# Attention with a residual: the place of the token loads in the transfer queue, and two exponentials ahead of a copy in one cycle

## The chip, the cores and the metric

The kernel runs on one core of a Trainium2 chip. The core's engines run side by side, each through its own list of instructions in order, and wait for each other through semaphores: TensorE (PE, matmuls; its weight loads are listed apart as PEld), VectorE (DVE), ScalarE (ACT), GpSimd (POOL) and SyncE (SP), which here only issues transfers (DMAs). The metric is the device time of one execution in microseconds (us). "Before" is the kernel without the change.

## What is computed

64 sequences of 128 tokens with 512 channels go through one attention block with 16 query heads and one shared key/value head of 64 channels, plus a null key and value, an additive bias per head, a causal mask and a padding mask. All is float32. Cut to what matters:

```python
xn = layernorm(x, g_in)
q = (xn @ Wq).reshape(b, n, H, DH).transpose(0, 2, 1, 3) * scale
kv = xn @ Wkv
k, v = (kv[..., :DH], kv[..., DH:])
k = concat([nk, k], axis=1); v = concat([nv, v], axis=1)
sim = einsum('bhid,bjd->bhij', q, k) + bias
sim = where(causal_mask, neg, sim); sim = where(mask_p, sim, neg)
attn = softmax(sim, axis=-1)
out = einsum('bhij,bjd->bhid', attn, v)
out = out.transpose(0, 2, 1, 3).reshape(b, n, INNER) @ Wo
return x + layernorm(out, g_out)
```

## The kernel before

The sequences are worked on in pairs. A hand-written prologue handles the first ones; then `cycle(c)` runs for c = 1 to 29, and a hand-written ending follows. In cycle c three things are interleaved: the softmax of the pair 2c and 2c + 1 (`scores_max`, `exps`, `rinv`, `scale`, `blocks_T`), the output product of the pair before (`values_out`, `out_sum`, `out_one`), and the layer norm and residual of the pair before that (`pair_...`, `store`). Query products (`q_one`, and from cycle 2 on `leaf`) and the key/value product (`key_values`) of later sequences fill TensorE. A cycle ends with `region(c)`: the scores of the next pair (line 651), `values` of the present pair (line 770), then the additions of scores and bias on VectorE. The matmuls of queries and outputs are lines 597, 553 and 860, those of keys and values line 358.

The order of every engine is the order in which the calls are written; nothing is rescheduled. `nc.tensor.addr_align` places TensorE's code at a set offset in each cycle.

The input tokens of a group of four sequences go through these steps. Their layer norm is applied on ScalarE (`norm_apply`), VectorE transposes them in blocks of 32 (`tokens_T`, into `xb`), and at the end of each even cycle up to 26 `tokens_out` stores `xb` to a buffer in main memory (`xd`, 1 MB, line 340) and `tokens_in` loads it back in another layout as `xT` (four loads of 256 KB, line 348). `xT` is read first by `key_values` in the odd cycle after it (line 358, `pkv`), later by the query products. Two buffers take turns for `xT`.

Also in the even cycles, `values_send` has VectorE transpose the values of a group (`vt`, line 384) and stores them to main memory (`vd`, two stores of 64 KB, line 387), and `keys_send` copies the keys to the upper half of the partitions (`kT`, 128 KB, line 393). `values_fetch` loads the values as `vr` (line 399) in the odd cycle that follows. `load_res` loads the tokens of one sequence for the residual (`res`, 256 KB, line 138) and `load_mask` a padding mask (line 145).

All of these transfers are issued by SyncE, in the order in which they are written, and an issue that must wait holds back those behind it. The program gives its transfers eight completion counters in turn (`DMAHW0` to `DMAHW7` in the order of instructions); an issue also waits until the transfer that had its counter last has landed.

In cycle 1 alone (c below `LEAF`, which is 2) the query products take another way: `q_one(c, 6, 0)` adds a product to a bank of PSUM (tag `a`) and `keep` copies it out on ScalarE (`ku`, line 608); `q_one(c, 7, 0)` then adds another to the same bank, and `q_one(c, 4, 0)` another, copied by line 614. `exps` (line 701) runs one exponential per head row of `S`, on ScalarE, each with a sum that is read out by an accumulator instruction.

Of the kernel before, what the change touches and what calls it, by code (L numbers as in the profile page):

```python
# [17 lines left out]
def kernel(  # L18
# [67 lines left out]
    GB = 4  # L86
# [257 lines left out]
    def tokens_in(g):  # L344
        xT[g] = gp.tile([P, GB, KC, N], FP, tag="xT", name=f"xT_{g}")
        xd = xds.pop(g).rearrange("(i p) j e -> j p i e", p=Q)
        for j in range(NQ):
            nc.sync.dma_start(
                out=xT[g][j * Q : (j + 1) * Q].rearrange("p i c n -> p i (c n)"),
                in_=xd[j],  # L350
            )
# [39 lines left out]
    def keys_send(g):  # L391

        nc.sync.dma_start(out=kT[g][DH:], in_=kT[g][:DH])
# [22 lines left out]
    def q_tile(g, fp):  # L416

        for h in range(2):
            slot = 2 * fp + h if g % 2 == 0 else fp + 2 * h
            qT[g, fp, h] = gp.tile(  # L420
                [P, FH, GH, NQ, 2, Q], FP, tag=f"q{slot}", name=f"qT_{g}_{fp}_{h}", bufs=1
            )

    def q_part(g, c, h):

        f = c % NF
        return qT[g, f // FH, h][:, f % FH, :, :, c // NF, :]
# [66 lines left out]
    LEAF = 2  # L494
# [4 lines left out]
    def by_block(tag):  # L499
        return prod[tag].rearrange("p (t i q) -> p t i q", t=2, i=NQ)  # L500

    def first_into(g, c, h):
        nc.scalar.copy(q_part(g, c, h), by_block("a"))  # L503
# [77 lines left out]
    def product(g, f, k, pool, tag, start=True):  # L581

        if start:
            prod[tag] = pool.tile([P, HT], FP, tag=tag, name=f"p{tag}_{g}_{f}_{k}")
        lo, hi = xT[g][:, 0 : GB // 2], xT[g][:, GB // 2 :]
        t1, t2, t3, t4 = (xS.get((g, i)) for i in range(1, 5))
        w, t = {
            1: (a11, lo[:, :, lo_k]),
            2: (a12, lo[:, :, hi_k]),
            3: (s4, hi[:, :, hi_k]),  # L590
            4: (a22, t4),
            5: (s1, t1),
            6: (s2, t2),
            7: (s3, t3),
        }[k]
        for kc in range(HK):
            nc.tensor.matmul(  # L597
                prod[tag],
                w[:, kc, f * P : (f + 1) * P],
                t[:, :, kc, :],  # L600
                start=(start and kc == 0),
                stop=(kc == HK - 1),
                skip_group_check=not start,
            )

    def keep(tag, name):
        kept[name] = bp.tile([P, HT], FP, tag=f"k{name}", name=f"k{name}", bufs=1)
        nc.scalar.copy(kept[name], prod[tag])

    def q_out(g, c, toks, tag, name=None):  # L610
        o = q_part(g, c, toks.start // HT)
        p = prod[tag].rearrange("p (t i q) -> p t i q", t=2, i=NQ)
        if name is None:
            nc.scalar.copy(o, p)
        else:
            k = kept.pop(name).rearrange("p (t i q) -> p t i q", t=2, i=NQ)
            nc.vector.tensor_tensor(o, p, k, ALU.add)
# [43 lines left out]
    def scores_upper(b, pool, tags):  # L661
        if len(tags) == 1:
            ps = pool.tile([P, 2, NF, N], FP, tag=tags, name=f"ps_{b}_1")
            heads(b, 1, [ps[:, r] for r in range(2)])
            pss[b, 1] = [(slice(0, R8), ps)]
        else:
            ps = [pool.tile([P, NF, N], FP, tag=t, name=f"ps_{b}_1{r}") for r, t in enumerate(tags)]
            heads(b, 1, ps)
            pss[b, 1] = [(slice(r * NF, (r + 1) * NF), ps[r]) for r in range(2)]

    def scores_lower(bs):
        low = [
            ps_q.tile([P, 2, NF, NL], FP, tag="ac"[r], name=f"ps_{bs[0]}_0{r}")
            for r in range(2)
        ]
        for k, b in enumerate(bs):
            heads(b, 0, [low[r][:, k] for r in range(2)])
            pss[b, 0] = [(slice(r * NF, (r + 1) * NF), low[r][:, k]) for r in range(2)]
# [3 lines left out]
    def scores_add(b, hf):  # L682
        for ks, ps in pss.pop((b, hf)):
            sv = S[b][:, ks, KEYS[hf]]
            if ks.stop - ks.start == R8:
                sv = sv.rearrange("p (r f) j -> p r f j", r=2)
            nc.vector.tensor_tensor(sv, ps, sv, ALU.add)  # L687

    def scores_max(b, hf):
        if hf == 0:  # L690
            nmax[b] = small.tile([P, 2, R8], FP, tag="nmax", name=f"nmax_{b}")
        nc.vector.tensor_reduce(  # L692
            nmax[b][:, hf], S[b][:, :, WITH_NULL[hf]], AX.X, ALU.max, negate=True
        )

    def exps(b, hf, lo=0, hi=R8):
        if hf == 0 and lo == 0:
            rsum[b] = small.tile([P, 2, R8], FP, tag="rsum", name=f"rsum_{b}")
        for k in range(lo, hi):
            row = S[b][:, k, WITH_NULL[hf]]  # L700
            nc.scalar.activation(  # L701
                row,
                row,
                AF.Exp,
                bias=nmax[b][:, hf, k : k + 1],
                accum_out=rsum[b][:, hf, k : k + 1],
            )
# [46 lines left out]
    def values(bs):  # L754
        banks = value_banks(bs[0])
        for k, b in enumerate(bs):
            values_one(b, k, banks)
# [222 lines left out]
    def q_one(c, k, h):  # L980
        i = 2 * c + 4 + h
        g, f = divmod(i, GB)
        if g >= NG:
            return
        if k == 1 and f % FH == 0:
            q_tile(g, f // FH)
        if k == 1:
            product(g, f, 1, ps_q, "a")
            if c >= LEAF:
                first_into(g, f, 0)  # L990
            else:
                keep("a", "p1")
        elif k == 2:
            product(g, f, 2, ps_w, "w")
            q_out(g, f, lo_t, "w", "p1")
        elif k == 5:
            product(g, f, 5, ps_q, "c")
        elif k == 6:
            product(g, f, 6, ps_q, "a", start=False)
            if c >= LEAF:  # L1000
                first_into(g, f, 1)
            else:
                keep("a", "u2")
        elif k == 7:
            product(g, f, 7, ps_q, "a", start=False)
            if c >= LEAF:
                first_into(g, HC + f, 0)
            else:
                keep("a", "u3")
                q_out(g, HC + f, hi_t, "c", "u3")  # L1010
        elif k == 8:
            nc.vector.tensor_tensor(
                q_part(g, HC + f, 1), by_block("c"), q_part(g, HC + f, 0), ALU.add
            )
            o = q_part(g, f, 1)
            nc.vector.tensor_tensor(o, by_block("c"), o, ALU.add)
        elif k == 3:
            product(g, f, 3, ps_q, "c", start=False)
            q_out(g, f, hi_t, "c", "u2")
        else:  # L1020
            product(g, f, 4, ps_q, "a", start=False)
            q_out(g, HC + f, lo_t, "a")
# [34 lines left out]
    def region(c):  # L1057
        b0, b1, n0, n1 = (2 * c + i for i in range(4))
        if n0 < B:
            scores_upper(n0, ps_s, "s")  # L1060
            scores_lower((n0, n1))
            scores_upper(n1, ps_w, "ww")
        if 0 <= b0 < B:
            values((b0, b1))
        if n0 < B:
            scores_add(n0, 1)
            scores_add(n0, 0)
            if c < 0:
                scores_max(n0, 0)
                scores_max(n0, 1)  # L1070
            scores_add(n1, 0)
            scores_add(n1, 1)
# [5 lines left out]
    def cycle(c):  # L1078
        b0, b1, n0, n1 = (2 * c + i for i in range(4))
        p, r, m = b0 - 2, b0 - 4, b0 + 10  # L1080
        soft, nxt = b0 < B, n0 < B
        pair, fin, toks = 0 <= p < B, 0 <= r < B, m < B
        first, more = c % 2 == 0, 2 * c + 4 < B
# [46 lines left out]
            q_one(c, 2, 0)  # L1130
        if c >= LEAF:
            leaf(c, 2, 0)
        q_one(c, 6, 0)
        if soft:
            exps(b0, 0)
        out_one(p, 1)
        if c % 2 and n0 < B:
            mask_neg(n0 // GB)
# [139 lines left out]
            tokens_out(m // GB)  # L1278
        if c >= LEAF:
            leaf(c, 3, 3)  # L1280
        if first and toks:
            tokens_in(m // GB)
        if pair:
            load_res(p)
        if first and send < NG:
            values_send(send)
            keys_send(send)
        region(c)


# [166 lines left out]
    for c in range(1, B // 2 - 2):  # L1457
        cycle(c)
# [186 lines left out]
```

## Time and profile before

| what | value |
|---|---|
| three runs | 1028.63, 1030.47, 1030.57 us (median 1030.47) |
| the profiled execution | 1028.7 us |
| its span, first to last instruction | 1026.9 us |
| mean granted TensorE clock | 0.998 |
| instructions | 31794 |
| ScalarE and GpSimd busy | 643.4 us (63%) and 790.5 us (77%) |
| VectorE busy | 854.6 us (83%) |
| transfers | 100.91 MB, mean 98 GB/s |

The profile is one execution, written by the hardware profiler. A row of a timeline or a group has the start in us from the span's start, the duration, the engine, the line of the kernel, the operation, the tile that is written and those that are read, and in brackets the time that the engine was idle before it and what ended that. "SPq" is SyncE's issue of a transfer: its duration is that of the issue, not of the transfer. A row of a stretch has the stretch, its length, then busy time and count of PE, PEld, DVE, ACT and POOL, the granted clock, the share of the transfer engines and GB/s. Queue q8 and q14 carry the engines' own instructions, q1 SyncE's transfers; a row of a queue has its packets, MB and the share of 16 transfer engines' time in the window asked for.

### The profile page before, as it was taken

How to read it: one execution, taken by the hardware profiler on the slowest of the kernel's cores; microseconds unless marked ns; L12 is line 12 of the kernel's file. 1: busy time of each engine (PE TensorE's matmuls, PEld its weight loads, DVE VectorE, ACT ScalarE, POOL GpSimd, SP SyncE). 2: the span in 40 equal slices, each digit the busy share in tenths (PEclk: the TensorE clock that was granted, in tenths of full speed). 3: DMA queues.
4: the chain of work that ended last, by engine and by line, in shares of the span. 5: the costliest groups of instructions: out<-in, count | busy, mean ns of one | idle time of the engine just before them, and what ended most of it. 6: DMA issues, size and time to landing. Idle time of an engine off the chain costs nothing. (4 is left out here: it accounts for less than half of the span.)

```text
span 1026.9 us, 31794 instructions
## 1 busy us (share of the span) xinstructions
PE 1011.5 (98%) x12104; PEld 898.8 (88%) x12104; DVE 854.6 (83%) x2000; ACT 643.4 (63%) x2742; POOL 790.5 (77%) x710
## 2 busy tenths in 40 slices
PE   8999999999999999999999999999999999999997
PEld 7888888888888899888889888898888898888876
DVE  6776888988888898888888889888888988778798
ACT  2655776555775556765557765557765567755591
POOL 3798959688695877968689596886968789596874
PEclk9999999999999999999999999999999999999999
DMA  6551251624314252241523505244151521402203
GB/s 212 164 128 52 95 126 40 160 64 134 106 39 142 64 154 87 80 121 43 168 74 99 132 32 158 64 125 115 44 153 48 157 85 72 109 26 68 84 2 103
DMA packets 70264, 100.91 MB, mean 98 GB/s; under 512 B 27744, under 2 KB 31328, under 8 KB 68320
## 3 DMA queue, kind: packets, MB, share of 16 engines
q1 hardware_dynamic: 69008, 97.83, 33.0%
q8 instruction: 96, 1.57, 0.7%
q10 hardware_dynamic: 1104, 1.05, 0.3%
q14 instruction: 56, 0.46, 0.2%
HBM read 63.19 MB, written 33.55 MB: 94 GB/s over the span
## 5 line engine op out<-in xcount | busy, mean ns | idle before, releaser
L701 ACT ACTIVATE s<-s,nmax 128x65 f32<-128x65 f32 (+1 forms) x1024 | 379.2, 409 | 3.5 <-DVE nmax L692 3.5
L701 ACT ACTIVATION_READ_ACCUMULATOR s<-s,nmax 128x1 f32 x1024 | 238.1, 233 | 0.0
L722 POOL TENSOR_TENSOR s<-s,rinv 128x1024 f32<-128x1024 f32 (+1 forms) x128 | 189.8, 1484 | 45.7 <-DVE rinv L718 45.7
L635 POOL TENSOR_TENSOR s<-biasp,mneg 128x1552 f32<-128x1552 f32 x64 | 205.1, 3224 | 2.6 <-DMA x<-in_x_dram 2.0
L810 ACT ACTIVATE oT<-poX,nv 128x256 f32<-128x256 f32 x58 | 27.6, 475 | 224.5 <-PE poX L770 117.5
L687 DVE TENSOR_TENSOR s<-ps,s 128x256 f32<-128x256 f32 (+2 forms) x224 | 120.0, 605 | 15.7 <-PE ps L651 15.2
L556 DVE TENSOR_TENSOR qT<-pl,qT 128x128 f32<-128x128 f32 (+1 forms) x420 | 122.5, 323 | 2.7 <-PE pl L553 2.3
L860 PE MATMUL pyX<-wo,oT 128*128 128x256 f32 x512 | 121.4, 380 | 0.0
L692 DVE TENSOR_REDUCE nmax<-s 128x8 f32<-128x520 f32 (+1 forms) x128 | 116.5, 949 | 0.1
L860 PE MATMUL pyX<-wT,oT 128*128 128x256 f32 x488 | 115.6, 380 | 0.7 <-POOL oT L843 0.7
L737 DVE STREAM_TRANSPOSE sb<-s 128x1536 f32<-128x1536 f32 x64 | 113.2, 1768 | 0.6 <-POOL s L722 0.6
L860 PEld LDWEIGHTS pyX<-wo,oT 128*128 128x128 f32 x512 | 96.9, 190 | 14.3 <-issue 0.9
L917 POOL TENSOR_TENSOR rstdo<-rstdo,nhalf 128x1 f32<-128x1 f32 x64 | 35.1, 550 | 86.5 <-DVE rstdo L913 86.5
L860 PEld LDWEIGHTS pyX<-wT,oT 128*128 128x128 f32 x488 | 88.3, 190 | 10.9 <-POOL oT L843 1.1
L651 PE MATMUL ps<-kT,qT 64*64 64x128 f32 (+1 forms) x4096 | 93.6, 245 | 0.7 <-issue 0.7
L651 PEld LDWEIGHTS ps<-kT,qT 64*64 64x64 f32 x4096 | 85.5, 134 | 5.7 <-issue 2.4
L770 PE MATMUL pos<-sb,vr 32*64 32x128 f32 (+1 forms) x1792 | 84.6, 322 | 2.1 <-issue 1.7
L843 POOL TENSOR_TENSOR yS<-oT 128x512 f32<-128x512 f32 x32 | 41.2, 1288 | 50.6 <-ACT oT L810 47.0
L770 PE MATMUL poY<-sb,vr 32*64 32x128 f32 x720 | 77.4, 349 | 0.0
L770 PE MATMUL poX<-sb,vr 32*64 32x128 f32 x960 | 75.6, 301 | 0.0
L718 DVE RECIPROCAL rinv<-rsum 128x8 f32<-128x8 f32 x128 | 23.8, 187 | 54.3 <-ACT s L701 54.2
L503 ACT COPY qT<-pa 128x256 f32<-128x256 f32 x168 | 67.9, 404 | 1.1 <-PE pa L597 1.1
(150 smaller groups left out, 2561.3 us busy)
## 6 DMA issues: line engine op xcount, KB each, us to landing
res<-in_x_dram SPq DMA_DIRECT2D x64, 256.0 KB, 3.0
out_dram<-y SPq DMA_DIRECT2D x58, 256.0 KB, 2.1
x<-in_x_dram SPq DMA_DIRECT2D x224, 64.0 KB, 2.0
xd<-xb SPq DMA_DIRECT2D x14, 1024.0 KB, 4.5
xT<-xd SPq DMA_DIRECT2D x56, 256.0 KB, 5.5
vr<-vd SPq DMA_DIRECT2D x64, 128.0 KB, 3.2
x<-in_x_dram SPq DMA_DIRECT2D x8, 256.0 KB, 4.8
vd<-vt SPq DMA_DIRECT2D x32, 64.0 KB, 5.9
```

Source lines behind the costliest of these rows:

```text
L503: nc.scalar.copy(q_part(g, c, h), by_block("a"))
L556: nc.vector.tensor_tensor(o, p, o, ALU.add)
L635: nc.gpsimd.tensor_tensor(S[b], biasp, mneg[:, t].unsqueeze(1).broadcast_to([P, R8, ROW]), ALU.add,)
L651: nc.tensor.matmul(to[r][i * DH : (i + 1) * DH, f, :], qT[g, f // FH, t // GH][rows, f % FH, t % GH, NQ - 1 - i if hf else i], kT[g][rows, ...
L687: nc.vector.tensor_tensor(sv, ps, sv, ALU.add)
L692: nc.vector.tensor_reduce(nmax[b][:, hf], S[b][:, :, WITH_NULL[hf]], AX.X, ALU.max, negate=True)
L701: nc.scalar.activation(row, row, AF.Exp, bias=nmax[b][:, hf, k : k + 1], accum_out=rsum[b][:, hf, k : k + 1],)
L722: nc.gpsimd.tensor_tensor(sv, sv, rinvs.pop((b, hf)).unsqueeze(2).broadcast_to([P, R8, sv.shape[2]]), ALU.mult,)
L737: nc.vector.transpose(sb.rearrange("p j e q -> p e j q"), S[b][:, :, 1 : ROW - 1].rearrange("p e (j k) -> p e j k", k=Q),)
L770: nc.tensor.matmul(po[s][rows, half], vr[g][quad(s), j, t, :], sb[quad(s), slots, r * NF : (r + 1) * NF, :], start=start, stop=True, skip_ ...
L843: nc.gpsimd.tensor_tensor(o, l, m, op)
L860: nc.tensor.matmul(prod[key], h[:, c, :], w[:, c, :], start=(start and c == 0), stop=(c == HC - 1), skip_group_check=not start,)
```

## The change

Two edits in `cycle`. In cycles that load tokens, `tokens_in` is called after `load_res`, `values_send` and `keys_send` instead of ahead of them. In cycle 1, where c is below `LEAF`, two of the eight exponentials of `exps(b0, 0)` are written ahead of `q_one(c, 6, 0)`; in the other cycles that order stays as it was.

```diff
-        q_one(c, 6, 0)
-        if soft:
-            exps(b0, 0)
+        if c >= LEAF:
+            q_one(c, 6, 0)
+        if soft:
+            exps(b0, 0, 0, 2)
+        if c < LEAF:
+            q_one(c, 6, 0)
+        if soft:
+            exps(b0, 0, 2, 8)
         out_one(p, 1)
...
-        if first and toks:
-            tokens_in(m // GB)
         if pair:
             load_res(p)
         if first and send < NG:
             values_send(send)
             keys_send(send)
+        if first and toks:
+            tokens_in(m // GB)
         region(c)
```

As the engines see it, first SyncE at the end of cycle 2, as it was. A row names the line, the tile written and those read, the shape, and the counters waited for (`DVE`, `PE`, `Pool` are the engines' own):

```order
L340 DMA xd_1592<-xb_1094 128x2048 [waits DMAHW3_49,DVE_49]
L348 DMA xT_1596<-xd_1592 32x4x512 [waits DMAHW3_49,DMAHW4_49,PE_49,Pool_49]
L348 DMA xT_1596<-xd_1592 32x4x512 [waits DMAHW5_49]
L348 DMA xT_1596<-xd_1592 32x4x512 [waits DMAHW6_49]
L348 DMA xT_1596<-xd_1592 32x4x512 [waits DMAHW7_49]
L138 DMA res_1601<-in_x_dram 128x512 [waits DMAHW0_49]
L387 DMA vd_1605<-vt_1603 512x1x32 [waits DMAHW1_49,DVE_49]
L387 DMA vd_1605<-vt_1603 512x1x32 [waits DMAHW2_49]
L393 DMA kT_1077<-kT_1077 64x512
L145 DMA m_3_1744<-in_mask_BxS_bk_dram 128x512 [waits DMAHW4_49]
```

and now:

```order
L340 DMA xd_1592<-xb_1094 128x2048 [waits DMAHW3_49,DVE_49]
L138 DMA res_1596<-in_x_dram 128x512 [waits DMAHW4_49]
L387 DMA vd_1600<-vt_1598 512x1x32 [waits DMAHW5_49,DVE_49]
L387 DMA vd_1600<-vt_1598 512x1x32 [waits DMAHW6_49]
L393 DMA kT_1077<-kT_1077 64x512 [waits DMAHW7_49,PE_49]
L348 DMA xT_1604<-xd_1592 32x4x512 [waits DMAHW0_49,DMAHW3_49,PE_49,Pool_49]
L348 DMA xT_1604<-xd_1592 32x4x512 [waits DMAHW1_49]
L348 DMA xT_1604<-xd_1592 32x4x512 [waits DMAHW2_49]
L348 DMA xT_1604<-xd_1592 32x4x512
L145 DMA m_3_1744<-in_mask_BxS_bk_dram 128x512 [waits DMAHW4_49]
```

The four loads of `xT` stand behind the residual load, the two value stores and the key copy, and no longer between the store of `xd`, for which they wait, and the residual load. The counters move with the places. The other even cycles up to 26 read the same way.

ScalarE in cycle 1 (`ku` is the copy of `keep`, `s` the scores, `rsum` their sums, `pa` the bank), before with -, now with +:

```order
 L810 ACTIVATE oT_946<-pos_869,nv_87 128x2x4x32 x2
-L608 COPY ku_979<-pa_2_1_958 128x256
-L701 ACTIVATE s_701,rsum_981<-s_701,nmax_949 128x65 x8
+L701 ACTIVATE s_701,rsum_977<-s_701,nmax_949 128x65 x2
+L608 COPY ku_982<-pa_2_1_958 128x256
+L701 ACTIVATE s_701,rsum_977<-s_701,nmax_949 128x65 x6
 L893 COPY kyp_995<-pyX_1_990 128x256
```

The copy stands behind two exponentials. The instructions of TensorE, VectorE and GpSimd keep their order.

## The prediction

> **What bounds the kernel now.** I read the page first: the share of each engine.
>
> ```profile
> span 1026.9 us, 31794 instructions
> PE 1011.5 (98%) x12104; PEld 898.8 (88%) x12104; DVE 854.6 (83%) x2000; ACT 643.4 (63%) x2742; POOL 790.5 (77%) x710
> ```
>
> TensorE (PE) is busy for 98% of the span, and the diff changes no matmul. So the edit can move the end only through time in which PE stands still. The view of waits, for PE, names few such times; the longest at a line that runs in every cycle:
>
> ```profile
> engine line waited for: us in total, times, longest us
> PE pos L770 <- issue: 1.7, 3, 1.0
> ```
>
> "issue" means that no semaphore explains the wait. These figures are too small, since the ends of matmuls are modelled: a stop shows whole only from start to start. So I took the starts of the cycles from the timeline (the first L597 matmul after the last L770 one; cycle 2 starts at 101.85, cycle 28 at 910.34) and asked for stretches between them: first three neighbours (cycles 8, 9 and 10), then the thirteen even cycles 2 to 26 in one call, of which I show the sum, then the thirteen odd cycles 3 to 27, again the sum.
>
> ```profile
> 288.32:320.56 32.24, 31.29 (x384) 27.88 (x378) 27.63 (x68) 20.20 (x86) 26.49 (x29) 1.00 0.39 117
> 320.56:351.46 30.90, 30.90 (x382) 27.71 (x379) 24.93 (x61) 20.17 (x86) 22.13 (x16) 1.00 0.28 79
> 351.46:382.36 30.90, 30.90 (x383) 27.72 (x379) 26.36 (x64) 20.19 (x86) 25.91 (x28) 1.00 0.36 109
> ...
> sum 406.52, PE 404.74 PEld 361.77 DVE 346.31 ACT 262.44 POOL 338.52; mean PE 31.13 PEld 27.83 DVE 26.64 ACT 20.19 POOL 26.04
> ...
> sum 401.97, PE 401.97 PEld 360.65 DVE 339.71 ACT 261.09 POOL 296.79; mean PE 30.92 PEld 27.74 DVE 26.13 ACT 20.08 POOL 22.83
> ```
>
> An undisturbed cycle takes 30.90 us, even or odd. Thirteen of them would be 401.70. The even cycles exceed that by 4.82 us, the odd ones by 0.27. The even cycles are those that issue `tokens_in`; something there stops PE. In cycle 8 the stop is one hole, in `values`:
>
> ```profile
> 316.95 0.27 PE L770 MATMUL poY<-sb,vr 32*64 32x128 f32 x2
> 318.18 0.32 PE L770 MATMUL pos<-sb,vr 32*64 32x128 f32 x2 [0.95 <-issue]
> ```
>
> From 316.95 to 318.18 nothing starts, and no semaphore is named. What else can a matmul lack? Its own instruction words. Queue q8, of kind "instruction", has 96 packets on the page (1.57 MB, 16 KB each) for 12104 matmuls and as many weight loads: 252 instructions a packet, 126 matmuls, three packets in a cycle of 378. I looked for the packet ahead of the hole through short windows of the view of transfers: cycle 8 (314.5 to 316.8), cycle 10 (377.1 to 378.1) and cycle 28 (936.35 to 937.65). The last column is the share of 16 engines, so 6.2% of 2.3 us is 2.28 us.
>
> ```profile
> q8 instruction: 1, 0.02, 6.2%
> ...
> q8 instruction: 1, 0.02, 6.0%
> ...
> q8 instruction: 1, 0.02, 5.9%
> ```
>
> It takes 0.96 us in cycle 10, from 25.7 us after the cycle's start, and 1.23 in cycle 28; in cycle 8 it starts at 26.2 and takes 2.28, until 316.8, and the hole follows. What it meets there is on SyncE's timeline, cycle 8 first, then the loads of cycle 10, then cycle 28:
>
> ```profile
> 307.80 0.42 SPq L138 DMA_DIRECT2D res<-in_x_dram  x1
> 308.69 0.34 SPq L340 DMA_DIRECT2D xd<-xb  x1
> 313.00 4.17 SPq L348 DMA_DIRECT2D xT<-xd  x4
> 317.22 0.43 SPq L138 DMA_DIRECT2D res<-in_x_dram  x1
> 317.75 1.55 SPq L387 DMA_DIRECT2D vd<-vt  x2
> 319.34 0.91 SPq L393 DMA_DIRECT2D kT<-kT  x1
> ...
> 376.59 2.83 SPq L348 DMA_DIRECT2D xT<-xd  x4
> ...
> 937.19 1.26 SPq L387 DMA_DIRECT2D vd<-vt  x2
> 938.50 0.63 SPq L393 DMA_DIRECT2D kT<-kT  x1
> ```
>
> The four token loads (1 MB) are issued from 24.7 us into cycle 8, just ahead of the packet. The read is: **the token loads delay the instruction packet that PE needs in `values`.** Cycle 10 loses nothing: its loads start 0.45 us later (25.1), and its packet is through before they crowd.
>
> **Part 1, the transfers.** Nothing is added or removed: in each of 13 even cycles four loads of 256 KB move behind one residual load (256 KB), two value stores (64 KB each) and one key copy (128 KB), all on SyncE's queue. When does each go out now? The residual load right behind `xd`, at 20.8 us into the cycle instead of 28.9: `xd` was issued at 308.69 and its data has landed when the first `xT` goes, at 313.00, so 4.3 us for 1 MB; another quarter costs about 1.1 us more, to about 25.5, still ahead of the packet at 25.7. The value stores wait for the transpose on VectorE:
>
> ```profile
> 314.44 0.71 DVE L384 STREAM_TRANSPOSE vt<-kT 64x512 f32<-64x512 f32 x1
> ```
>
> It ends 26.8 us into the cycle. The queue stands there from 21.2 to 26.8; behind it are only the key copy and the token loads, and no other transfer was issued in these 5.6 us before either, but the loads. Value stores and key copy take 1.26 + 0.63 us to issue (cycle 28), so the loads start at about 28.8 instead of 24.7, and go on to 30.7. The waits that are added on the counters of the queue's lanes fall on transfers of the cycle's middle, landed by then: nothing.
>
> So the packet at 25.7 meets no token loads. Cycle 28 is nearly the new order, stores at 26.9 without token loads ahead. The stretches of cycle 12 and of cycle 28:
>
> ```profile
> 413.26:444.42 31.16, 31.16 (x384) 27.88 (x379) 26.62 (x64) 20.19 (x86) 25.96 (x28) 1.00 0.38 111
> ...
> 910.34:941.25 30.91, 30.91 (x384) 27.75 (x379) 23.59 (x54) 18.90 (x84) 24.65 (x26) 1.00 0.16 46
> ```
>
> Cycle 28 is 0.01 us over the clean one. I take that as the value for the even cycles, and add the 0.27 of the odd ones for the residual load that now sits close by: gain 4.82 − 0.27 = **4.55 us**. Bounds: at best all 4.82; at worst each of the 13 keeps the 0.26 us that cycle 12 shows (31.16 against 30.90), 3.4 in all, and the gain is 1.4.
>
> Where does the collision go? On the next packet, wanted about 126 matmuls after the hole. Counted on the timeline, that is in the first group here, 5.5 us or more into cycle 9 (36.4 from the start of an undisturbed even cycle). Behind it stand the first reader of the loaded tokens and that next packet, undisturbed (411.5 to 412.8, cycle 11) and in the old order (320.0 to 321.2):
>
> ```profile
> 326.07 1.89 PE L860 MATMUL pyw<-wo,oT 128*128 128x256 f32 x8
> ...
> 329.33 1.89 PE L358 MATMUL pkv<-xT,wkv 128*128 128x256 f32 x8
> ...
> q8 instruction: 1, 0.02, 5.7%
> ...
> q8 instruction: 1, 0.02, 5.8%
> ```
>
> Undisturbed it comes 29.2 us into a cycle and takes 1.2; behind cycle 8's loads it came at 31.7, and no odd cycle stops for it. A delay like that of cycle 8's first packet (0.5 later, 1.3 longer) puts it down by 32.2, against 36.4 wanted. The tokens are read 8.8 us into the odd cycle, 39.7 from the even cycle's start. The loads land 6.9 us after issue in cycle 8 (median, view of transfers), so the last, issued at 30.2, by 37.1, some 2.6 us early.
>
> ```profile
> xT<-xd SPq DMA_DIRECT2D x4, 256.0 KB, 6.9
> ```
>
> The mask load and the value fetch go out behind the loads, in the first microseconds of the odd cycle; the fetched values are read in the even cycle after it.
>
> The Trainium skill (Runtime: NRT & Kernel Launch, Instruction fetch mechanics) says that instructions come in 16 KiB blocks over a DMA queue of the sequencer's own while the block before runs, and that a boundary is mostly hidden. The trace agrees on the size and not on the hiding. By that rule the reorder would give nothing; that is the second rival below, 1028.4.
>
> **Part 2, two exponentials of cycle 1.** They go ahead of the copy `u2`. ScalarE now, then PE, then the maxima that the exponentials need:
>
> ```profile
> 73.02 0.37 ACT L608 COPY ku<-pa 128x256 f32<-128x256 f32 x1 [0.35 <-ACT oT L810]
> 73.29 0.35 ACT L701 ACTIVATE s<-s,nmax 128x65 f32<-128x65 f32 x1
> 73.63 0.34 ACT L701 ACTIVATE s<-s,nmax 128x65 f32<-128x65 f32 x1
> ...
> 78.80 0.37 ACT L614 COPY qT<-pa 128x256 f32<-128x256 f32 x1
> ...
> 74.50 1.03 PE L597 MATMUL pa<-xS,wq 128*128 128x256 f32 x4
> ...
> 77.09 1.03 PE L597 MATMUL pa<-xS,wq 128*128 128x256 f32 x4
> 77.95 1.03 PE L597 MATMUL pc<-xT,wS 128*128 128x256 f32 x4
> 79.22 1.13 PE L597 MATMUL pa<-xT,wq 128*128 128x256 f32 x4 [0.23 <-ACT qT L614]
> ...
> 68.76 3.55 DVE L692 TENSOR_REDUCE nmax<-s 128x8 f32<-128x520 f32 x4
> ```
>
> ScalarE idles 0.35 us before the copy, from 72.67, when all four maxima stand (72.31). Exponentials go out every 0.34 us, so two take 0.68; the copy starts about 0.33 later, at 73.35, and ends by 73.7. The next matmul on its bank is at 74.50: 0.8 us of cover, so nothing. All that follows on ScalarE comes 0.33–0.35 us earlier, down to the L614 copy that PE waits for at 79.22. Four matmuls take 0.86 us from start to start (77.09 to 77.95), so PE could have gone on at 78.82; it stood 0.40. Gain **0.33 us**, bounds 0 and 0.40. If the copy's cover were gone, the loss would be the two exponentials less the idle gap, 0.33.
>
> **Sum.** Against the profiled execution, 1028.7 us (span 1026.9 plus 1.8 around it): 1028.7 − 4.55 − 0.33 = 1023.8. That execution is at the low end of the runs shown (1028.63 to 1030.57, median 1030.47). Were the other runs' 1.8 us more of the same stops, they would go too; were they something else, the median would be 1025.6. I take 1024.3, nearer the first, because these stops are what varies from cycle to cycle (0 to 1.34 us).
>
> **Rivals.** *The stores take the loads' place.* Value stores and key copy now go out from 26.9, with the packet still under way in slow cycles. For it: a store has 512 rows of 128 bytes by its shape. Against: cycle 28 has just this and loses 0.01. Then each even cycle keeps about 0.26: 1028.7 − 1.4 − 0.3 = 1027.0, or 1028 at the median's level.
>
> *The fetch is hidden and the hole has another cause* in the region, which stays. For: cycle 12 loses 0.26 with no wait named. Against: odd cycles have the same matmuls and 0.27 in all. Only part 2 is left: 1028.4 (1030.1 by the median).
>
> *Slower: the loads come too late.* The place is `pkv` in the odd cycle, 39.7 us from the even cycle's start; the point from which it decides is a landing later than that, over 9 us after the last issue at 30.2. In cycle 8 the landing took 6.9 in a crowd. Now the crowd behind them is the value fetch, four more loads. Each us beyond costs 13, once per even cycle: 2 us beyond gives 1023.8 + 26 = 1050, and less than 0.4 beyond is lost in the gain.
>
> **How the numbers follow.** Forecast (stops gone) 0.80; stores in the loads' place 0.08; hole stays 0.06; loads too late 0.06. 0.2% of the time is 2 us, about what a measurement tells from no change: faster means under 1028.4, slower above 1032.5. The forecast is faster throughout, the second case in most of its chance, the third is no change, of the fourth most is slower: 0.86, 0.09, 0.05. The range: below, all 4.82, the 0.40 and the odd cycles' 0.27 gone is 1023.2, and 0.4 for the scatter of the runs (the three shown lie 0.1 to 1.9 apart) makes 1022.8. Above, the second case on the profiled level, 1027.0. That leaves out the last two rivals and half of the second.
>
> **What would show it.** Right: even cycles 2 to 26 at 30.9 to 31.0; the "issue" waits of L770 down to that of cycle 1; the token loads issued about 28.8 us into the cycle, the q8 packet at 25.7 taking about 1 us; the wait of L597 for L614 gone and cycle 1 shorter by 0.3. Wrong: holes of the old size in `values` with a quiet q8 packet (third case), or a new PE wait at `pkv` on the `xT` transfer (fourth).

## The result, and the profile after

| what | before | changed |
|---|---|---|
| median of 17 runs each | 1029.97 us | 1023.67 us |
| lowest and highest | 1024.32 and 1034.18 | 1023.20 and 1024.96 |
| profiled execution, span | 1028.7, 1026.9 us | 1023.2, 1021.4 us |

The ratio is 0.9945, with a 95% interval of 0.9933 to 0.9956. The changed kernel is faster by 0.4 to 0.7%, 1023.67 against 1024.3 forecast, inside the range. Its runs also lie within 1.8 us, where those of before spread over 10.

The page of the changed kernel, then its view of PE's waits (line waited at, releaser, us in total, times, longest):

```profile
span 1021.4 us, 31818 instructions
PE 1008.8 (99%) x12104; PEld 897.8 (88%) x12104; DVE 852.9 (84%) x2000; ACT 643.1 (63%) x2742; POOL 790.9 (77%) x710
```

```profile
PE pos L770 <- issue: 0.3, 1, 0.3
```

Three waits, 1.7 us together, have become one of 0.3. The wait of L597 for the L614 copy is not in this list any more. Where the time came from shows in the stretches between starts of cycles: here cycles 2 and 8, then the sum of the thirteen even cycles 2 to 26, then that of the odd cycles 3 to 27.

```profile
100.97:132.18 31.21, 31.21 (x384) 27.80 (x379) 26.14 (x62) 20.18 (x86) 27.04 (x29) 1.00 0.35 99
286.67:317.57 30.90, 30.90 (x384) 27.72 (x379) 26.36 (x64) 20.19 (x86) 25.94 (x28) 1.00 0.32 99
sum 402.00, PE 402.00 PEld 360.40 DVE 342.39 ACT 262.39 POOL 338.39; mean PE 30.92 PEld 27.72 DVE 26.34 ACT 20.18 POOL 26.03
...
sum 402.00, PE 402.00 PEld 360.55 DVE 342.33 ACT 261.11 POOL 297.31; mean PE 30.92 PEld 27.73 DVE 26.33 ACT 20.09 POOL 22.87
```

The even cycles went from 406.52 to 402.00, by 4.52 us; the odd ones stayed (401.97). All that is left over 401.70 is in cycle 2 (31.21). Cycle 8 lost its hole: 32.24 became 30.90. Its transfers on SyncE's timeline, and the two instruction packets of PE near them, in windows of the view of transfers from 312.3 to 313.5 and from 315.9 to 317.2 (last column: share of 16 engines):

```profile
307.04 0.34 SPq L340 DMA_DIRECT2D xd<-xb  x1
307.43 0.43 SPq L138 DMA_DIRECT2D res<-in_x_dram  x1
313.53 1.25 SPq L387 DMA_DIRECT2D vd<-vt  x2
314.87 0.71 SPq L393 DMA_DIRECT2D kT<-kT  x1
315.76 2.71 SPq L348 DMA_DIRECT2D xT<-xd  x4
```

```profile
q8 instruction: 1, 0.02, 5.5%
...
q8 instruction: 1, 0.02, 5.8%
```

The first packet takes 5.5% of 16 × 1.2 us, 1.06 us, and lies before 313.5, with hardly anything else under way. The token loads go out from 315.76, 29.1 us into the cycle. The second packet takes 1.2 us, as in a quiet cycle.

In cycle 1, ScalarE and then PE:

```profile
72.16 0.41 ACT L701 ACTIVATE s<-s,nmax 128x65 f32<-128x65 f32 x1
72.49 0.40 ACT L701 ACTIVATE s<-s,nmax 128x65 f32<-128x65 f32 x1
72.82 0.42 ACT L608 COPY ku<-pa 128x256 f32<-128x256 f32 x1
...
77.92 0.39 ACT L614 COPY qT<-pa 128x256 f32<-128x256 f32 x1
```

```profile
77.62 1.03 PE L597 MATMUL pc<-xT,wS 128*128 128x256 f32 x4
78.48 1.03 PE L597 MATMUL pa<-xT,wq 128*128 128x256 f32 x4
```

The L597 group follows its neighbour after 0.86 us, with no wait.

The balance of the profiled executions: span shorter by 5.5 us = 4.5 (even cycles) + 0.55 (cycle 1: 32.64 to 32.09) + 0.34 (the prologue, which the change doesn't touch: cycle 1 starts at 68.88 instead of 69.22, and the forecast had nothing for it) + 0.1 elsewhere.

### The profile page after: what moved, and what is told of

Its sections match the earlier page's. It is cut to its first block, busy times and chain, and to the rows that moved or that the text cites. A ratio compares the mean times of both kernels' runs of the same rounds, so it can differ in the third digit from the quotient of the medians.

```text
span 1021.4 us, 31818 instructions
## 1 busy us (share of the span) xinstructions
PE 1008.8 (99%) x12104; PEld 897.8 (88%) x12104; DVE 852.9 (84%) x2000; ACT 643.1 (63%) x2742; POOL 790.9 (77%) x710
## 5 line engine op out<-in xcount | busy, mean ns | idle before, releaser
L810 ACT ACTIVATE oT<-poX,nv 128x256 f32<-128x256 f32 x58 | 27.5, 475 | 220.0 <-PE poX L770 113.0
L770 PE MATMUL pos<-sb,vr 32*64 32x128 f32 (+1 forms) x1792 | 82.1, 321 | 0.3 <-issue 0.3
L770 PE MATMUL poY<-sb,vr 32*64 32x128 f32 x720 | 74.9, 347 | 0.0
L860 PE MATMUL pyw<-wo,oT 128*128 128x256 f32 x280 | 66.4, 380 | 0.5 <-POOL oT L843 0.5
```

What stands on the lines that cost most here:

```text
L770: nc.tensor.matmul(po[s][rows, half], vr[g][quad(s), j, t, :], sb[quad(s), slots, r * NF : (r + 1) * NF, :], start=start, stop=True, skip_ ...
L860: nc.tensor.matmul(prod[key], h[:, c, :], w[:, c, :], start=(start and c == 0), stop=(c == HC - 1), skip_group_check=not start,)
```

## Experiments

The theory to test: the token loads, at the moment when they went out, made an instruction packet of TensorE late, and `values` stood still for it. In the sums below 401.70 is thirteen times 30.90. Each ratio is to runs of the kernel before that were made beside the experiment (their medians lie between 1027.5 and 1029.4 us), so the ratios compare better than the times.

**Each part alone.** `e1`: the diff's second half alone; `e2`: its first half alone.

> Only the token loads are moved behind the residual load, the value stores and the key copy; the exponentials stay as they were. Theory (the loads delayed the instruction packet): nearly all of the gain, ratio to before about 0.995, even cycles 4 to 26 at 30.90 us, and 0.3 us above the changed kernel. Rival (the two exponentials or the prologue bring a good part of it): ratio above 0.998.

> Only the two exponentials of cycle 1 are moved. Theory: the even cycles keep their holes (13 of them together 2 to 8 us over 401.70), the wait of L597 for L614 in cycle 1 is gone and cycle 1 is shorter by about 0.35 us than its 32.64; the time can't be told from that of before (within 0.2%). Rival (the exponentials set off all later cycles differently): a clear gain of 2 us or more.

`e1`: 1023.58 us, ratio 0.9952 (0.9935 to 0.9968). `e2`: 1029.11, ratio 1.001 (0.9995 to 1.0024). The sums of the even cycles, `e1` first, then `e2`:

```profile
sum 402.26, PE 402.26 PEld 360.70 DVE 342.42 ACT 262.26 POOL 337.75; mean PE 30.94 PEld 27.75 DVE 26.34 ACT 20.17 POOL 25.98
```

```profile
sum 407.67, PE 404.24 PEld 361.45 DVE 347.72 ACT 262.25 POOL 339.10; mean PE 31.10 PEld 27.80 DVE 26.75 ACT 20.17 POOL 26.08
```

The transfers bring the gain, and the exponentials leave the holes where they were (6.0 us). Not all of `e1` went as expected: two of its even cycles, 12 and 18, still lose a quarter of a microsecond, with no token load near. This is cycle 12:

```profile
410.78:441.93 31.15, 31.15 (x384) 27.88 (x379) 26.61 (x64) 20.18 (x86) 25.93 (x28) 1.00 0.34 99
```

So a loss of this size doesn't need the token loads. Of the larger ones (0.5 to 1.34 us in before) none is left. What the early exponentials bring is too small for the times: the two medians of `e1` and of the change can't be told apart. In the traces it is plain: from cycle 1's start to its first score matmul PE needs 26.11 us in all four profiled kernels that have the exponentials early (the change, `e2`, `e5`, `e6`), and 26.60 to 26.62 in the eight without. That is 0.51 us, where the expectation had 0.35.

**Which transfer it is.** `e3` puts the token loads behind the residual load only:

```diff
-        if first and toks:
-            tokens_in(m // GB)
         if pair:
             load_res(p)
+        if first and toks:
+            tokens_in(m // GB)
         if first and send < NG:
```

> The token loads go behind the residual load alone, ahead of the value stores and the key copy; exponentials as before. Their issue still follows the landing of xd, so it stays at about 24.7 to 25.5 us into the even cycle, with the residual load out at 20.8 as in the changed kernel. Theory (the moment of the token loads counts): holes remain, time of before within 0.2% (1027 to 1031). Rival (the early residual load, or its no longer coming behind the loads, is what helps): the time of the changed kernel, 1024.

The expectation missed: 1024.29 us, ratio 0.9961 (0.9946 to 0.9976), most of the gain. Cycle 10 on SyncE's timeline, then the sum of the even cycles:

```profile
369.78 0.34 SPq L340 DMA_DIRECT2D xd<-xb  x1
370.17 0.43 SPq L138 DMA_DIRECT2D res<-in_x_dram  x1
375.00 2.47 SPq L348 DMA_DIRECT2D xT<-xd  x4
```

```profile
sum 403.06, PE 402.97 PEld 360.92 DVE 343.68 ACT 262.22 POOL 338.26; mean PE 31.00 PEld 27.76 DVE 26.44 ACT 20.17 POOL 26.02
```

1.36 us of holes are left of 4.82. The loads go out a little later than before, on average 25.26 us into the even cycle against 24.97, since `xd` now shares its time with the residual load. So either a few tenths of a microsecond in the moment of the loads decide, or the early residual load does. `e7` has the residual load last (`xd`, value stores, key copy, token loads, residual); `e8` has it in the middle of each cycle, behind `load_x(m + 2)`, with the token loads right behind `xd` as before.

```diff
         if first and send < NG:
             values_send(send)
             keys_send(send)
+        if first and toks:
+            tokens_in(m // GB)
+        if pair:
+            load_res(p)
         region(c)
```

```diff
         if m + 2 < B:
             load_x(m + 2)
+        if pair:
+            load_res(p)
...
         if first and toks:
             tokens_in(m // GB)
-        if pair:
-            load_res(p)
```

> The token loads go behind the value stores and the key copy, but the residual load stays behind them all, as before (order: xd, value stores, key copy, token loads, residual); exponentials as before. Theory (the moment of the token loads counts; they go out at about 28.8 us into the even cycle): even cycles near 30.90, time of the transfers moved alone, 1023.6 (ratio to before 0.995). Rival (the early residual load is what helped when the loads went behind it alone): holes as before, ratio within 0.2% of 1.

> The residual load of the first sequence goes out in the middle of every cycle, about 14 us into it, with its data long landed when xd is stored; the token loads stay right behind xd, ahead of the value stores, and go out at about 24.7 us as before; exponentials as before. Theory (moment of the token loads): holes of the even cycles remain, together 2 to 8 us, ratio within 0.2% of 1. Rival (early residual load): holes gone, ratio about 0.995.

`e7`: 1024.33 us, ratio 0.996 (0.9944 to 0.9975). `e8`: 1027.20, ratio 0.9989 (0.998 to 0.9999). Their sums, `e7` first:

```profile
sum 402.37, PE 402.37 PEld 360.60 DVE 342.54 ACT 262.40 POOL 338.39; mean PE 30.95 PEld 27.74 DVE 26.35 ACT 20.18 POOL 26.03
```

```profile
sum 405.87, PE 403.92 PEld 361.41 DVE 345.75 ACT 262.41 POOL 338.98; mean PE 31.07 PEld 27.80 DVE 26.60 ACT 20.19 POOL 26.08
```

With the residual load last and the token loads late 0.7 us of holes are left; with it early and the token loads in their old place 4.2 us remain. The residual load's own place is not the cause. In `e8` the token loads go out at 25.01 on average, almost as before. That leaves the moment of the loads, which `e9` and `e10` try in the order of before: one or two copies of 256 KB from main memory to main memory, read by nobody, right behind `xd` (`e10` has `range(2)`).

```diff
         if first and toks:
+            for i in range(1):
+                nc.sync.dma_start(
+                    out=dp.tile([P, DIM], FP, tag=f"more{i}", name=f"more_{c}_{i}"),
+                    in_=x[m + i],
+                )
             tokens_in(m // GB)
```

> Kernel before with one added copy of 256 KB from main memory to main memory (read by nobody) issued right behind xd in the even cycles; everything else in its old place, the residual load last. The copy shares the transfer engines with xd, as the residual load does when the loads go behind it, so the token loads should go out 0.2 to 0.6 us later than before. Theory (a few tenths of a microsecond in the moment of the token loads decide): holes of the even cycles fall to 0 to 2 us together, ratio to before 0.996 to 0.998. Rival (the delay doesn't matter, and the place of the residual load does): holes as before, 3 us and more, ratio 0.998 to 1.002.

> The same with two such copies, 512 KB, and the token loads 0.6 to 1.5 us later than before, at 25.5 us and more into the cycle. Theory: holes as small as with one copy or smaller, 0 to 1 us together, ratio 0.995 to 0.997, unless the copies themselves still run when the instruction packet comes at 25.7; then the packet is late by them and the holes grow again. Rival (place of the residual load): holes as before, ratio 0.998 to 1.002.

`e9`: 1024.91 us, ratio 0.9972 (0.996 to 0.9985). `e10`: 1026.83, ratio 0.9995 (0.9984 to 1.0006). Sums, `e9` first:

```profile
sum 402.77, PE 402.72 PEld 360.73 DVE 342.84 ACT 262.40 POOL 337.89; mean PE 30.98 PEld 27.75 DVE 26.37 ACT 20.18 POOL 25.99
```

```profile
sum 404.65, PE 404.21 PEld 361.70 DVE 344.68 ACT 262.41 POOL 337.86; mean PE 31.09 PEld 27.82 DVE 26.51 ACT 20.19 POOL 25.99
```

One added copy of useless data makes the kernel faster than before: the loads go out at 25.33 us on average, and the holes fall to 1.1. With two copies the loads go out hardly later still (25.42), but the data of the copies run until 26.2 on average (25.5 with one copy), past the 25.7 at which a quiet packet starts; the instruction packets start at 26.1 on average instead of the 25.9 of `e9`, and 2.95 of holes are back, as the expectation allowed. So the moment of the loads isn't the rule by itself. The reading that fits all of these runs is that the engines must be free when the packet comes.

**Is it the instruction packet?** `e4` is the kernel before with TensorE's code shifted by 32 instructions, so that each boundary of a packet comes 16 matmuls earlier.

```diff
-            nc.tensor.addr_align(256, offset={1: 120, B // 2 - 3: 76}.get(c, 94))
+            nc.tensor.addr_align(256, offset={1: 120, B // 2 - 3: 76}.get(c, 126))
```

> Kernel before, with TensorE's code shifted by 32 instructions (16 matmuls with their weight loads) in cycles 2 to 28: offset 126 instead of 94, so that every packet's boundary comes 16 matmuls earlier. Theory (the hole is a late instruction packet): the hole of the even cycles moves 16 matmuls earlier, from the 15th matmul of values to the end of the scores (L651). Rival (a data transfer, a bank or the values themselves make the hole): it stays at the same matmul of L770.

The time, 1057.45 us, is no measure of this: 15 us are lost in cycle 29, most of them in one stop of 13.7 us in which TensorE runs through padding (the trace has 584 empty instructions, NOP, instead of 328). The holes are what counts. Cycle 3 on PE's timeline, then the sum of the even and that of the odd cycles:

```profile
135.38 0.60 PE L597 MATMUL pa<-xS,wS 128*128 128x256 f32 x2
137.29 0.59 PE L597 MATMUL pa<-xS,wS 128*128 128x256 f32 x2 [1.31 <-issue]
```

```profile
sum 402.55, PE 401.96 PEld 360.15 DVE 342.45 ACT 262.52 POOL 335.65; mean PE 30.92 PEld 27.70 DVE 26.34 ACT 20.19 POOL 25.82
...
sum 419.31, PE 403.74 PEld 360.18 DVE 342.50 ACT 263.18 POOL 296.70; mean PE 31.06 PEld 27.71 DVE 26.35 ACT 20.24 POOL 22.82
```

The hole left `values` altogether. It didn't go where I expected, to the end of the scores: the packet for that boundary now comes at 24.2 us, ahead of the token loads, and the even cycles are clean but for cycle 2. A hole now stands ahead of matmul 12 of each odd cycle (counted from 0 by start), in the middle of one product. In the kernel before the hole stood ahead of matmul 279 of a cycle of 378; the next boundary, 128 matmuls on, is matmul 29 of the next cycle, and 16 earlier is 13, one off what is found. So holes move with the code's address, which no cause in data or in a bank would do. This hole belongs to the second packet, which the loads of the even cycle make late; in the kernel before it was wanted some 16 matmuls, about 3.5 us, later and so cost nothing.

**Does any bulk transfer do it?** `e6` is the changed kernel with an added store of 768 KB in each odd cycle from 3 on, of data that VectorE has just written.

```diff
+        if not first and c > 1:
+            nc.sync.dma_start(
+                out=dp.tile([P, 6 * R8 * Q], FP, tag="more", name=f"more_{c}"),
+                in_=sbs[b1].rearrange("p j e q -> p (j e q)"),
+            )
```

> Changed kernel with an added store in each odd cycle from 3 on: the transposed probabilities of the pair's second sequence (768 KB, read by nobody) to main memory, issued when VectorE has written them, about 24.5 us into the cycle, where odd cycles had no transfer. Theory (any bulk transfer ahead of the instruction packet makes the hole): the odd cycles get holes of 0.25 us and more in values, together 2 to 12 us over 30.90 each, and the time rises by as much. Rival (only the token loads do it, by the buffer that they read or write): odd cycles stay at 30.90, time within 0.2% of the changed kernel.

1038.85 us, ratio to before 1.0092 (1.0074 to 1.011), 15.3 us more in the profiled span than the change. Cycle 9's store, the packet (window 346.9 to 348.0), the hole, and the sum of the odd cycles:

```profile
343.68 0.33 SPq L1289 DMA_DIRECT2D more<-sb  x1
```

```profile
q8 instruction: 1, 0.02, 5.3%
```

```profile
348.28 0.27 PE L770 MATMUL pos<-sb,vr 32*64 32x128 f32 x1
349.35 0.27 PE L770 MATMUL pos<-sb,vr 32*64 32x128 f32 x1 [0.80 <-issue]
```

```profile
sum 414.05, PE 406.08 PEld 361.89 DVE 353.20 ACT 261.10 POOL 304.03; mean PE 31.24 PEld 27.84 DVE 27.17 ACT 20.08 POOL 23.39
```

The clean odd cycles now lose 12.35 us, just above the 2 to 12 expected, within one matmul of where the even cycles of before lost theirs; the even ones stay at 402.0, and another 3.7 us go in cycle 29, which has the store too. Buffer and direction differ from the token loads, so a bulk transfer of another kind does it too. The packet of cycle 9 takes 0.94 us, as in a quiet cycle, but starts 27.3 us into the cycle instead of 25.7.

**How late may the loads go?** `e5` is the changed kernel with the token loads behind the value fetch of the odd cycle.

```diff
         if not first and fetch < NG:
             values_fetch(fetch)
+        if not first and c > 2 and m - 2 < B:
+            tokens_in((m - 2) // GB)
```

> Changed kernel, but the token loads go out in the odd cycle, behind the value fetch, some 1.5 to 3.5 us into it; they land about 5.2 us after issue, 7 to 9 us into it, where pkv reads them at 8.8. Theory: the even cycles stay free of holes, and the margin of the slower rival shows: a wait of PE at pkv of 0 to 1 us in each odd cycle, 1023.5 to 1037. Rival (the loads have far more room than that): no wait, 1023.7.

1039.40 us, ratio 1.0088 (1.0069 to 1.0107). Cycle 9, first on SyncE, then on PE, and the sum of the odd cycles:

```profile
324.32 1.84 SPq L348 DMA_DIRECT2D xT<-xd  x4
```

```profile
332.44 1.10 PE L358 MATMUL pkv<-xT,wkv 128*128 128x256 f32 x4 [0.62 <-DVE mv L286]
```

```profile
sum 417.76, PE 404.76 PEld 361.28 DVE 345.82 ACT 263.44 POOL 300.56; mean PE 31.14 PEld 27.79 DVE 26.60 ACT 20.26 POOL 23.12
```

Each odd cycle waits at `pkv`, together 16.1 us; the wait named is VectorE's, which had long been done; in the view of waits 5.6 us of those at `pkv` are put down to the `xT` transfer. The landings settle it: in all thirteen odd cycles `pkv` starts 0.1 to 0.25 us behind the landing of the last `xT` load (in cycle 9 at 9.55 us, the landing at 9.41). The wait of 1.2 us on average is more than the 0 to 1 us that was expected, and the time is above the 1037 at most. So the slower rival is real: loads that go out some 1 to 3.5 us into the odd cycle are too late, those of the change, whose issue in cycle 8 ends 0.9 us into it, are not.

## Why the prediction was right

**The bound.** PE alone, through its stops, set what could be won; the balance above accounts for the span with no other engine.

**Part 1, forecast 4.55 us, measured 4.52.** The step "the token loads delay the instruction packet" is shown in three independent ways: holes move with the code's address (`e4`), appear where another transfer is put (`e6`), and all but 0.6 to 0.7 us go when the transfers alone are moved (`e1`, `e7`). The trace of before says the same cycle by cycle: the four even cycles that lose nothing have their packet down 26.6 to 27.1 us into the cycle, the nine that lose time 27.1 to 28.5. Cycle 28 was the right model for the new order, though one clean cycle was thin ground: in `e1` and `e7` cycle 28 itself loses 0.29 and 0.23. The even cycles except cycle 2 are at 30.9, and the residual load's data were through 25.1 to 25.9 us into the cycles, about when the packet starts. In cycle 8 the loads went out at 29.1 rather than 28.8, and their issue lasted 2.7 us rather than 1.9, into the odd cycle. The next packet was hardly delayed there, less than I allowed.

That the two figures agree to 0.03 us is luck. The 0.27 taken off was meant for the residual load beside the packet; what is left is 0.3 in cycle 2 alone, where the residual load is through before the packet starts, and `e1`, with the same transfers, has 0.56 left.

What I didn't see is how narrow the matter was: I priced the whole reorder, and loads that go out 0.3 to 0.4 us later on average bring most of it (`e3`, `e9`). In before, cycle 10 shows how little room there is:

```profile
377.07 2.91 PE L651 MATMUL ps<-kT,qT 64*64 64x128 f32 x128
```

The packet starts as these 128 matmuls, a packet's worth, do (25.7 and 25.6 us into the cycle), and it is wanted at 28.64. My reason for cycle 10's escape, loads 0.45 us later than in cycle 8, is only a tendency: all five cycles that lose 0.5 us or more have their loads out by 24.90, but cycles 22 and 24, with loads at 24.93 and 24.97, lose nothing, and cycle 16, at 25.10, loses 0.26.

**Part 2, forecast 0.33 us, measured 0.51, beyond its bound of 0.40.** The mechanism was right, the term mis-sized twice. ScalarE's idle time before the copy was taken from the end of the row ahead (72.67); but instructions there overlap, and the first exponential starts 3.28 us into the cycle, 0.52 ahead of the copy's old start (3.80). So the L614 copy came 0.54 earlier in the cycle (9.04 instead of 9.58), enough for the whole of PE's 0.40. And the group that followed the stop had run longer: at 79.22 it took 1.13 us, at 78.48 it takes 1.03. That row stood in the prediction, and I passed over the 0.10.

**The median.** I chose 1024.3 on the ground that the extra time of the slower runs was more of the same stops. The runs of the change agree: their spread went from 10 us to 1.8. Only the profiled executions show holes one by one, so for the others this is an inference.

**The rivals.** *Stores in the loads' place*: not seen, twelve of thirteen even cycles lose nothing. *Hole from another cause*: refuted by `e4` and `e6` for the large holes. *Loads too late*: not so here; the last load lands 36.6 to 38.0 us after the even cycle's start, against 39.7 wanted, so in the worst cycle 1.6 us were left instead of 2.6. `e5` shows the price, some 1.2 us for each odd cycle, with the loads some 3 to 4 us later than in the change.

**Still open.** Cycle 2 keeps 0.31 us, and cycle 1 loses 0 to 0.7 us in `values` from kernel to kernel, with no transfer issued near it. Single cycles of `e1` and `e7` lose 0.2 to 0.3 with no token load near (in cycle 8 of `e7` the packet starts at 26.38 all the same). Four of before's nine stops, 1.1 us together, are of this size, and they may not all be due to the loads. What delays the packets there wasn't tried. No version that beats the changed kernel came out of these runs.

## What to carry to other kernels

When TensorE stops with "issue" as the reason, look for its instruction packets in the view of transfers, and for the bulk transfer that was issued just before. On an engine that streams much code, place bulk transfers by the moments of its packets: half a microsecond can decide here, and a transfer that isn't needed soon belongs behind the one that waits for something. Matmul ends are modelled, so compare starts of like stages, cycle by cycle, before believing that 98% busy leaves nothing.

## What the runs showed of the hardware that was not expected

PE resumed about 1.4 us after the late packet's end, not at once: packet down at 316.80 and PE at 318.18 before (1.38), 347.9 and 349.35 in `e6` (1.44). It isn't a fixed time: in the nine even cycles of before that lost time it was 0.83 to 1.67. There the line between packets that cost nothing and packets that cost time lies at about 1.5 us before they are wanted (28.64 us into the cycle).

A packet of 16 KB that takes 0.9 to 1.4 us with no bulk transfer beside it took up to 2.28 behind the token loads, and started up to 1.8 us late behind the store in `e6` (27.5 us into the cycle instead of 25.7).
